# Pre-norm attention and an fp8 feed-forward on one core: softmax reciprocals by exp(-ln) on ACT, elementwise work of the rounds on DVE

## The chip, the core and the metric

The kernel runs on one core of a Trainium2 chip. A core has a matrix engine (TensorE, in the profile PE, with weight loads as PEld), a vector engine (VectorE, DVE), an engine for activation functions (ScalarE, ACT), a general one (GpSimd, POOL) and one that here only starts transfers (SyncE, SP). Each works through its own queue of instructions in order; semaphores tie the queues together. SBUF is the memory on the chip, PSUM the banks that TensorE writes. The metric is the device time of one execution in microseconds. The kernel before took 1808.78 us as the median of three runs (1807.12 to 1813.49).

## What is computed

```python
x = x + attention(layernorm(x))       # x: 2 x 2048 x 512, float32
x = x + ffn(layernorm(x))

# attention: 16 heads of 32, 2 groups of keys and values
q = rope(xn @ wq + bq) * 32 ** -0.5
k = rope(xn @ wk + bk); v = xn @ wv + bv
attn = softmax(q @ k.T * 32 ** -0.5)   # over 2048 keys
out = (attn @ v) @ wo + bo

# ffn: xn and the weight are each scaled to a maximum of 448 and rounded to e4m3
out = bf16((x_fp8 @ w_fp8.T) * (x_scale * w_scale))
```

The softmax is computed as a product of unnormalized probabilities with v, times the reciprocal of their sum.

## The kernel before

The 4096 tokens are 8 blocks of 512. Each block has 4 quads (4 heads each), and each quad two halves of 256 queries: 64 *units*. A unit goes through the 2048 keys of its batch in 16 chunks of 128, four chunks to a *round*, so there are 4 rounds in a unit and 256 in all.

In a round, `probabilities` (L969, L978, L987) does each chunk: TensorE writes the scores of 4 heads of a chunk into one of two PSUM tiles T (parity E or O), on top of the negated maxima of the queries for the first two chunks (the tile mT times `sel`, L969; later chunks add differences of keys to what stands in the tile), and ACT takes exp to SBUF as p. DVE adds p in pairs (`add_pair`, L961), an accumulating DMA issued from POOL's queue adds pair to pair (L991), and DVE joins what results (L994). TensorE multiplies p with the values one round later (`columns`, L924) and the joined sums with a tile of ones (`sum_up`, L942), which gives the sum of probabilities in the same layout as the values' product. Both lie in one tile `avs`, two buffers of it.

For the next unit, `first_scores` (L509, L517) and `gather_maxima` (L490, L529, L533) give the maxima of a first set of keys; the transposed maxima are copied by ACT to mT in the last round of a unit, between the second and the third chunk.

`finish_heads` (L890) ends a unit while the next one runs: ACT copies the sums out of PSUM (L895), DVE takes their largest bit pattern into `seen` (L897) and their reciprocal in two pieces (L903), POOL multiplies (L904) into `attn_of`. `seen` is compared with a bound at the very end (L1157); above it a slower general path would compute everything once more.

Beside the units run *jobs*, generators that yield ON_PE, ON_DVE, OTHER or LATER: the projection of keys and values of a later block (`project_kv`, `stack_keys`), of queries (`project_q`, `turn`, `rope`), the output product (`finish_block`), and the second norm. `fill` (called four times a round) takes the next piece of a job whose kind fits; LATER puts the rest off to the next round. The place of an instruction in each engine's queue is fixed by this order when the program is written out. `attending` is true in the rounds and false in the front part, which prepares the first keys and queries, and in the tail, which does the feed-forward.

In the rounds, these elementwise steps are on POOL: the two of `rope` (L325, L326), the difference `lo` in `halves` (L237), the difference of keys (L410), the copy of the old keys (L377), and var and mean of a norm (L196, L197). The normalizing of a block (`normalize`) is two activations on ACT in the rounds (L250, L253) and one DVE operation outside of them (L257).

Of the kernel before, what the change touches and what calls it, by code (L numbers as in the profile page):

```python
# [8 lines left out]
F32 = mybir.dt.float32  # L9
F32R = mybir.dt.float32r  # L10
BF16 = mybir.dt.bfloat16
U32 = mybir.dt.uint32
AF = mybir.ActivationFunctionType
ALU = mybir.AluOpType
AX = mybir.AxisListType

P = 128
# [3 lines left out]
TB = 512  # L21
NT = TB // P
EPS = 1e-5
# [4 lines left out]
def preln_attn_fp8_ffn_kernel(  # L28
# [37 lines left out]
    nc = tc.nc  # L66
# [9 lines left out]
    HB = 256  # L76
# [5 lines left out]
    ON_PE, ON_DVE, OTHER = "PE", "DVE", "other"  # L82
    LATER = "later"
# [101 lines left out]
    def layernorm_stats(src, mean, rstd, name, tiles=range(NT)):  # L185

        stats = small.tile([P, NT, 6], F32, tag="stats", name=f"stats_{name}")
        mv = small.tile([P, NT, 2], F32, tag="mv", name=f"mv_{name}")
        for i in tiles:
            yield ON_DVE  # L190
            nc.vector.bn_stats(stats[:, i, :], src[:, i, :])
            nc.vector.bn_aggr(mv[:, i, :], stats[:, i, :])
        at = slice(tiles[0], tiles[-1] + 1)
        var = small.tile([P, NT], F32, tag="var", name=f"var_{name}")
        engine = nc.gpsimd if attending[0] else nc.vector
        engine.tensor_scalar(var[:, at], mv[:, at, 1], EPS, None, ALU.add)  # L196
        engine.tensor_copy(mean[:, at], mv[:, at, 0])  # L197
        nc.gpsimd.tensor_tensor(rstd[:, at], var[:, at], neg_half[:, at], ALU.pow)
        if attending[0]:
            yield LATER  # L200
            yield OTHER
            yield LATER
# [15 lines left out]
    def round_e4m3(dst, v, magic):  # L218
# [10 lines left out]
        nc.vector.tensor_tensor(v, v, magic, ALU.add)  # L229
        nc.vector.tensor_tensor(dst, v, magic, ALU.subtract)  # L230

    def halves(src, rows, name):

        hi = t2(f"hi_{name}", F32R)
        lo = t2(f"lo_{name}", F32R)
        nc.scalar.copy(hi[:rows], src)
        nc.gpsimd.tensor_tensor(lo[:rows], src, hi[:rows].bitcast(F32), ALU.subtract)  # L237
        return hi, lo


# [3 lines left out]
    def normalized(n, xt, xnT, name):  # L244


        def normalize(i):
            if attending[0]:
                xn = t2(f"xn_{name}_{i}")
                nc.scalar.activation(  # L250
                    xn, xt[:, i, :], AF.Identity, bias=neg_mean[:, i : i + 1]
                )
                nc.scalar.activation(xn, xn, AF.Copy, scale=rstd1[:, n, i : i + 1])  # L253
                return xn
            else:
                xn = ppool.tile([P, 2, TB], F32, tag="p", name=f"xn_{name}_{i}")[:, 0, :]
            nc.vector.tensor_scalar(  # L257
                xn,
                xt[:, i, :],
                mean1[:, n, i : i + 1],  # L260
                rstd1[:, n, i : i + 1],
                ALU.subtract,
                ALU.mult,
            )
            return xn

        if attending[0]:
            neg_mean = small.tile([P, NT], F32, tag="neg_mean", name=f"neg_mean_{name}")
            nc.scalar.mul(neg_mean, mean1[:, n, :], -1.0)
        for i in range(0, NT, 2):  # L270
            xn = {}
            for h in (i, i + 1):
                yield OTHER if attending[0] else ON_DVE
                xn[h] = normalize(h)
            for h in (i, i + 1):
                yield ON_PE
                tp = bank(f"tp_{name}_{h}")
                for c in range(DC):
                    nc.tensor.transpose(
                        tp[:, c * P : (c + 1) * P], xn[h][:, c * P : (c + 1) * P], ident  # L280
                    )
                nc.scalar.copy(
                    xnT[:, :, h * P : (h + 1) * P], tp.rearrange("p (c t) -> p c t", c=DC)
                )
                give_back()
# [36 lines left out]

    def rope(dst, q, u, rows, csb):

        nc.gpsimd.tensor_tensor(q[:rows], q[:rows], csb[:rows, 0, :], ALU.mult)  # L325
        nc.gpsimd.tensor_tensor(dst, u[:rows], q[:rows], ALU.add)  # L326

# [34 lines left out]
    def project_kv(n, xt, xnT, csb):  # L364
        b, blk = divmod(n, NB)
        yield from layernorm_stats(xt, mean1[:, n, :], rstd1[:, n, :], f"1_{n}")
        yield from normalized(n, xt, xnT, f"kv_{n}")
        if n > 0:
            nc.sync.dma_start(xnT_far[n], xnT)
        if b not in vX:  # L370
            vX[b] = wide.tile([P, NTS, GROUPS, HD], F32, tag="vX", name=f"vX_{b}", bufs=2)
        pk = bank(f"pk_{n}")
        yield from product(pk, lambda c: wkv_sb[:, c, :], lambda c: xnT[:, c, :])
        if blk == 0:
            nc.gpsimd.memset(kx[:, :BACK], 0.0)
        else:
            nc.gpsimd.tensor_copy(kx[:, :BACK], kx[:, TB:])  # L377
        kv = t2(f"kv_{n}")
        nc.scalar.activation(kv, pk, AF.Identity, bias=bkv_sb)
        give_back()  # L380
        if attending[0]:
            u = swapped(kv, KD, f"k_{n}")
        else:
            u = yield from rotated(kv, csb, f"k_{n}")
        yield ON_PE
        tv = bank(f"tv_{n}")
        for i in range(NT):
            nc.tensor.transpose(tv[:, i * P : (i + 1) * P], kv[:, i * P : (i + 1) * P], ident)
        nc.scalar.copy(
            vX[b][:, blk * NT : (blk + 1) * NT, :, :].rearrange("p i g d -> p i (g d)"),  # L390
            tv.rearrange("p (i k) -> p i k", i=NT)[:, :, KD:],
        )
        give_back()
        if attending[0]:
            beside.insert(0, Job(stack_keys(n, kv, u, csb), due=step[0] + 2))
        else:
            yield from stack_keys(n, kv, u, csb)

    def stack_keys(n, kv, u, csb):
        b, blk = divmod(n, NB)  # L400
        if attending[0]:
            yield ON_DVE
            rotate(u, csb, KD)
        rope(kx[:, BACK:], kv, u, KD, csb)
        if attending[0]:
            table_users[0] -= 1
        cols = slice(blk * TB, (blk + 1) * TB)
        yield OTHER
        src = t2(f"dk_{n}")[:KD]
        nc.gpsimd.tensor_tensor(src, kx[:, BACK:], kx[:, :TB], ALU.subtract)  # L410
        if attending[0]:
            yield LATER
            yield OTHER
        far = halves_far["dkS", b]
        for h, part in enumerate(halves(src, KD, f"dkS_{n}")):
            nc.sync.dma_start(far[:, h, cols], part[:KD].bitcast(F32))
        if b == 0:
            far = far.rearrange("(g d) h t -> d h g t", g=GROUPS)
            stack(
                lambda rows: stacked["dkS"][rows, :, cols],  # L420
                [far[:, h, :, cols] for h in (0, 0, 1, 1)],
            )
        keys_done.add(n)
# [422 lines left out]
    def ask(u):  # L846
# [39 lines left out]
        if n == NBLK - 1 and quad == 3 and half == 0:  # L886

            fetch_y(4, wide, "qst", bufs=2)
            fetch_y_over_keys(5, "dkS", 0)

    def finish_heads(u, both, sums):

        k, half = units[u]
        n, quad = quads[k]
        nc.scalar.copy(both[:, 1, :], sums)  # L895
        yield ON_DVE
        nc.vector.tensor_reduce(  # L897
            seen[:, u : u + 1], both[:, 1, :].bitcast(U32), AX.X, ALU.max
        )
        for c in range(HB // P):  # L900
            yield ON_DVE
            piece = both[:, 1, c * P : (c + 1) * P]
            nc.vector.reciprocal(piece, piece)  # L903
        nc.gpsimd.tensor_tensor(  # L904
            attn_of[n][:, quad, half * HB : (half + 1) * HB], both[:, 0, :], both[:, 1, :], ALU.mult
        )
        if n == NBLK - 1:
            if quad == QUADS - 2 and half == HALVES - 1:
                queue.append(Job(finish_most(n, x_res[n], attn_of[n])))
            elif quad == QUADS - 1:  # L910
                queue.append(Job(finish_rest(n, x_res[n], attn_of[n], half)))
        elif quad == QUADS - 1 and half == HALVES - 1:
            job = Job(finish_block(n, attn_of.pop(n)))
            if n not in biased:
                job.due = NEVER
                without_x[n] = job
            queue.append(job)
# [90 lines left out]
        columns(u, chunks, probs, unit.avs[:, 0, :])  # L1008

    def keep_values(unit):  # L1010
        unit.both = w2.tile([P, 2, HB], F32, tag="both", name=f"both_{unit.u}", bufs=2)
        nc.scalar.copy(unit.both[:, 0, :], unit.avs[:, 0, :])  # L1012

    with tc.manual_schedule():
# [139 lines left out]
            ready = ahead  # L1154

    top = small.tile([P, 1], F32, tag="top", name="top")
    nc.vector.tensor_reduce(top, seen, AX.X, ALU.max)  # L1157
    across = bank("across_seen")
    nc.tensor.transpose(across[:1, :P], top, ident)
    flag = small.tile([1, 1], mybir.dt.int32, tag="flag", name="flag")  # L1160
# [264 lines left out]
```

## Time and profile before

| what | value |
|---|---|
| median of the runs | 1808.78 us |
| profiled execution, its own time | 1806.86 us |
| its span | 1805.0 us |
| granted clock of TensorE, mean | 0.966 |
| rounds | from about 92 to 1693 us |
| front part | about 92 us |
| tail | about 110 us |

Times in the profile are those of one execution on the chip. A line of a group of instructions gives the line of the source, the engine, the operation, what it writes and reads with the shapes, the count, the busy time with the mean of one in ns, and then the idle time of the engine just before them with what ended it. A line of the timeline gives the start, the length, the engine, and in brackets the idle time before it; instructions that follow one another are merged, so a length can hold several. A line of a stretch gives the stretch, its length, the busy time of PE, PEld, DVE, ACT and POOL with counts, the granted clock as a share of full speed, the DMA engines' share and GB/s. Matmuls overlap and their ends are modelled.

### The profile page before, as it was taken

The page shows a single profiled execution, that of the slowest core. Times are in us where ns is not written, and L with a number is a line of the kernel's source. Part 1 is how long each engine was busy: PE and PEld are TensorE (multiplying, and loading weights), DVE is VectorE, ACT ScalarE, POOL GpSimd, SP SyncE. Part 2 cuts the span into 40 slices and gives each one's busy share as a digit, 9 for nine tenths or more (in the row PEclk, how much of TensorE's full clock was granted, in tenths as well). Part 3 has the DMA queues.
Part 4 walks back from the last instruction along what each step waited for, and adds up shares of the span by engine and source line. Part 5 has one row for each costly group of instructions (what it writes and reads, how often), then busy time and mean ns, then how long its engine had stood idle before and what let it go on. Part 6 is the DMA issues. An engine that isn't in the chain of part 4 may idle for free.

```text
span 1805.0 us, 33804 instructions
## 1 busy us (share of the span) xinstructions
PE 1598.6 (89%) x13483; PEld 916.2 (51%) x13483; DVE 1315.7 (73%) x1526; ACT 1208.3 (67%) x1473; POOL 545.2 (30%) x552
## 2 busy tenths in 40 slices
PE   5588999899998999898999998999899988899664
PEld 3254555555555555555555554555555545555322
DVE  4547787767876787767768777787878787577697
ACT  2167677876767776776766777767777667566365
POOL 2333333244322532243314222332324223122100
PEclk9699999999999999999999999999999999999878
DMA  5676676767577866767588567766677558776222
GB/s 187 175 165 134 155 151 152 179 147 158 119 189 168 171 131 150 196 157 160 121 206 167 123 141 175 161 145 128 135 186 155 120 132 182 146 183 140 64 82 107
DMA packets 105431, 272.65 MB, mean 151 GB/s; under 512 B 15536, under 2 KB 16176, under 8 KB 102576
## 3 DMA queue, kind: packets, MB, share of 16 engines
q0 software_dynamic: 40944, 142.10, 42.1%
q1 hardware_dynamic: 61904, 126.92, 23.3%
q8 instruction: 108, 1.77, 0.4%
q10 hardware_dynamic: 2416, 1.38, 0.2%
q14 instruction: 59, 0.48, 0.1%
HBM read 87.36 MB, written 40.89 MB: 71 GB/s over the span
## 4 chain that ended last, share of the span: by engine, by line
PE 50%; DVE 14%; DMA 12%; issue 10%; ACT 7%; POOL 4%; SPq 2%; ACTq 0%; DVEq 0%; POOLq 0%
PE T L978 17%; PE avs L924 16%; DMA pa<-pa 9%; ACT p L987 6%; PE po L291 5%; DVE pa L961 4%; PE pq L291 3%; PE avs L942 2%; PE T L969 2%; DVE pa L994 2%; SPq L304 2%; DMA sw_q<-q 2%; PE pk L291 2%; PE s L509 1%; DVE v L229 1%
## 5 line engine op out<-in xcount | busy, mean ns | idle before, releaser
L987 ACT ACTIVATE p<-T 128x1024 f32<-128x1024 f32 x1024 | 991.9, 1023 | 218.1 <-PE T L978 214.3
L961 DVE TENSOR_TENSOR pa<-p,p 128x1024 f32<-128x1024 f32 x511 | 687.6, 1348 | 383.0 <-ACT p L987 273.2
L978 PE MATMUL T<-qst,dkS 128*128 128x512 f32 x2048 | 688.2, 446 | 44.8 <-ACT p L987 44.4
L991 POOL DMA_DIRECT2D pa<-pa x255 | 221.0, 867 | 971.8 <-DVE pa L961 671.6
L924 PE MATMUL avs<-p,vX 128*32 128x256 f32 x8192 | 497.3, 383 | 0.0
L978 PEld LDWEIGHTS T<-qst,dkS 128*128 128x128 f32 x2048 | 343.7, 191 | 285.2 <-ACT p L987 157.6
L924 PEld LDWEIGHTS avs<-p,vX 128*32 128x32 f32 x8192 | 240.4, 110 | 228.0 <-issue 96.5
L994 DVE TENSOR_TENSOR pa<-pa,pa 128x1024 f32<-128x1024 f32 x125 | 169.8, 1358 | 0.0
L291 PE MATMUL po<-wo_sb,attn 128*128 128x512 f32 x256 | 126.1, 604 | 0.0
L903 DVE RECIPROCAL both<-both 128x128 f32<-128x128 f32 x128 | 121.4, 949 | 5.6 <-DVE seen L897 0.5
L969 PE MATMUL T<-mT,sel 128*128 128x256 f32 x512 | 102.7, 324 | 11.2 <-ACT p L987 10.7
L291 PE MATMUL pq<-xnT_q,wq_sb 128*128 128x512 f32 x224 | 112.1, 607 | 0.0
L942 PE MATMUL avs<-pa,ones 128*32 128x256 f32 x1048 | 81.5, 385 | 28.7 <-DVE pa L994 27.7
L969 PEld LDWEIGHTS T<-mT,sel 128*128 128x128 f32 x512 | 78.0, 193 | 46.0 <-issue 20.6
L509 PEld LDWEIGHTS s<-dkS,qst 128*128 128x128 f32 x512 | 79.0, 196 | 22.2 <-DVE mx L517 10.9
L517 DVE TENSOR_REDUCE mx<-s 128x4 f32<-128x512 f32 x128 | 87.4, 683 | 2.8 <-PE s L509 2.8
L1012 ACT COPY both<-avs 128x256 f32<-128x256 f32 x64 | 23.9, 373 | 90.8 <-PE avs L942 88.1
L509 PE MATMUL s<-dkS,qst 128*128 128x128 f32 x512 | 74.4, 269 | 9.4 <-DVE mx L517 9.4
L904 POOL TENSOR_TENSOR attn<-both 128x256 f32<-128x256 f32 x64 | 78.9, 1232 | 9.7 <-DVE both L903 9.7
L895 ACT COPY both<-avs 128x256 f32<-128x256 f32 x64 | 23.9, 373 | 84.8 <-PE avs L942 84.8
L326 POOL TENSOR_TENSOR q<-sw_q,q 128x512 f32<-128x512 f32 x30 | 54.7, 1825 | 38.3 <-DVE sw_q L309 37.9
L533 ACT CAST mT<-mtp 128x256 fp32r<-128x256 f32 x64 | 23.8, 372 | 56.5 <-PE mtp L529 56.5
(124 smaller groups left out, 1075.5 us busy)
## 6 DMA issues: line engine op xcount, KB each, us to landing
pa<-pa POOLq DMA_DIRECT2D x255, 512.0 KB, 5.0
qst<-q_far SPq DMA_DIRECT2D x128, 256.0 KB, 4.9
q_far<-hi_q SPq DMA_DIRECT2D x32, 256.0 KB, 2.8
q_far<-lo_q SPq DMA_DIRECT2D x32, 256.0 KB, 3.4
x_res<-in_L_attn_x_dram SPq DMA_DIRECT2D x16, 512.0 KB, 7.2
x_res<-in_L_attn_bo_dram POOLq DMA_DIRECT2D x8, 1024.0 KB, 12.7
out_dram<-v SPq DMA_DIRECT2D x16, 512.0 KB, 2.8
sw_q<-q SPq DMA_DIRECT2D x240, 32.0 KB, 3.6
```

The costliest lines, as they stand in the source:

```text
L291: nc.tensor.matmul(dst, lhs(c), rhs(c), start=(c == 0), stop=(c == chunks - 1))
L509: nc.tensor.matmul(s[:, j, :], qst[k][:, j, at : at + P], stacked["dkS"][:, group(k), :FIRST], start=True, stop=True, skip_group_check=True,)
L517: nc.vector.tensor_reduce(mx[:, i, :], s, AX.X, ALU.max)
L903: nc.vector.reciprocal(piece, piece)
L924: nc.tensor.matmul(av[j * HD : (j + 1) * HD, :], vX[batch(k)][:, kc, group(k), :], p[:, j, :], start=(kc == 0), stop=(kc == NTS - 1), tile ...
L942: nc.tensor.matmul(dst[j * HD : (j + 1) * HD, :], ones, part[:, j, :], start=start and i == 0, stop=stop and i == len(parts) - 1, tile_pos ...
L961: nc.vector.tensor_tensor(pa, a, b, ALU.add)
L969: nc.tensor.matmul(T[:, j, :], sel[:, j, :], maxima[u], start=(j % 2 == 0), stop=True, skip_group_check=True,)
L978: nc.tensor.matmul(T[:, j : j + 2, :], stacked["dkS"][:, group(k), kc * P : (kc + 1) * P], qst[k][:, j : j + 2, half * HB : (half + 1) * H ...
L987: nc.scalar.activation(p, T, AF.Exp, scale=SCALE)
L991: nc.gpsimd.dma_start(out=to, in_=of, accum_op=ALU.add)
L994: nc.vector.tensor_tensor(to, to, of, ALU.add)
```

## The change

Three things change.

- `finish_heads` no longer uses DVE's reciprocal. ACT copies the sums and accumulates them along the row into `seen` in the same instruction. A round later ACT takes Ln of the sums s and Exp of its negative, which is a guess g of 1/s. Another round later DVE does a Newton step, (s g - 2) g, which is the negated refined reciprocal, and multiplies with the values and with -1. The tile `both` has three parts in place of two.
- The guard at the end takes the bit pattern of those row sums.
- In the rounds, what POOL did elementwise (the two rope operations, `lo`, the difference and the copy of keys, var and mean) is on DVE, and so is the normalizing, which ACT did in two activations. POOL keeps the power -1/2 of the variance, small operations of the second norm, and its DMA issues. The pieces concerned ask for a DVE slot (ON_DVE).

```diff
-        engine = nc.gpsimd if attending[0] else nc.vector
-        engine.tensor_scalar(var[:, at], mv[:, at, 1], EPS, None, ALU.add)
-        engine.tensor_copy(mean[:, at], mv[:, at, 0])
+        nc.vector.tensor_scalar(var[:, at], mv[:, at, 1], EPS, None, ALU.add)
+        nc.vector.tensor_copy(mean[:, at], mv[:, at, 0])
...
+    def elementwise():
+
+        return nc.vector if attending[0] else nc.gpsimd
+
     def halves(src, rows, name):
...
-        nc.gpsimd.tensor_tensor(lo[:rows], src, hi[:rows].bitcast(F32), ALU.subtract)
+        elementwise().tensor_tensor(lo[:rows], src, hi[:rows].bitcast(F32), ALU.subtract)
...
                 xn = t2(f"xn_{name}_{i}")
-                nc.scalar.activation(
-                    xn, xt[:, i, :], AF.Identity, bias=neg_mean[:, i : i + 1]
-                )
-                nc.scalar.activation(xn, xn, AF.Copy, scale=rstd1[:, n, i : i + 1])
-                return xn
...
-                yield OTHER if attending[0] else ON_DVE
+                yield ON_DVE
...
-        nc.gpsimd.tensor_tensor(q[:rows], q[:rows], csb[:rows, 0, :], ALU.mult)
-        nc.gpsimd.tensor_tensor(dst, u[:rows], q[:rows], ALU.add)
+        elementwise().tensor_tensor(q[:rows], q[:rows], csb[:rows, 0, :], ALU.mult)
+        elementwise().tensor_tensor(dst, u[:rows], q[:rows], ALU.add)
...
-            nc.gpsimd.tensor_copy(kx[:, :BACK], kx[:, TB:])
+            elementwise().tensor_copy(kx[:, :BACK], kx[:, TB:])
...
-        nc.gpsimd.tensor_tensor(src, kx[:, BACK:], kx[:, :TB], ALU.subtract)
+        elementwise().tensor_tensor(src, kx[:, BACK:], kx[:, :TB], ALU.subtract)
...
-        nc.scalar.copy(both[:, 1, :], sums)
+        av, total, guess = (both[:, i, :] for i in range(3))
+        nc.scalar.activation(total, sums, AF.Copy, accum_out=seen[:, u : u + 1])
+        yield LATER
         yield ON_DVE
-        nc.vector.tensor_reduce(
-            seen[:, u : u + 1], both[:, 1, :].bitcast(U32), AX.X, ALU.max
-        )
-        for c in range(HB // P):
-            yield ON_DVE
-            piece = both[:, 1, c * P : (c + 1) * P]
-            nc.vector.reciprocal(piece, piece)
-        nc.gpsimd.tensor_tensor(
-            attn_of[n][:, quad, half * HB : (half + 1) * HB], both[:, 0, :], both[:, 1, :], ALU.mult
+        nc.scalar.activation(guess, total, AF.Ln)
+        nc.scalar.activation(guess, guess, AF.Exp, scale=-1.0)
+        yield LATER
+        yield ON_DVE
+        nc.vector.tensor_tensor(total, total, guess, ALU.mult)
+        nc.vector.scalar_tensor_tensor(total, total, 2.0, guess, ALU.subtract, ALU.mult)
+        nc.vector.scalar_tensor_tensor(
+            attn_of[n][:, quad, half * HB : (half + 1) * HB], av, -1.0, total, ALU.mult, ALU.mult
         )
...
-        unit.both = w2.tile([P, 2, HB], F32, tag="both", name=f"both_{unit.u}", bufs=2)
+        unit.both = w2.tile([P, 3, HB], F32, tag="both", name=f"both_{unit.u}", bufs=2)
...
-    nc.vector.tensor_reduce(top, seen, AX.X, ALU.max)
+    nc.vector.tensor_reduce(top, seen.bitcast(U32), AX.X, ALU.max)
```

More of the change, by code (lines that the diff above doesn't have):

```diff
@@ L265, in normalize @@
             return xn
-        if attending[0]:
-            neg_mean = small.tile([P, NT], F32, tag="neg_mean", name=f"neg_mean_{name}")
-            nc.scalar.mul(neg_mean, mean1[:, n, :], -1.0)
         for i in range(0, NT, 2):
@@ L407, in stack_keys @@
         cols = slice(blk * TB, (blk + 1) * TB)
-        yield OTHER
+        yield ON_DVE
         src = t2(f"dk_{n}")[:KD]
-        nc.gpsimd.tensor_tensor(src, kx[:, BACK:], kx[:, :TB], ALU.subtract)
+        elementwise().tensor_tensor(src, kx[:, BACK:], kx[:, :TB], ALU.subtract)
         if attending[0]:
@@ L894, in finish_heads @@
         n, quad = quads[k]
-        nc.scalar.copy(both[:, 1, :], sums)
+        av, total, guess = (both[:, i, :] for i in range(3))
+        nc.scalar.activation(total, sums, AF.Copy, accum_out=seen[:, u : u + 1])
+        yield LATER
         yield ON_DVE
-        nc.vector.tensor_reduce(
-            seen[:, u : u + 1], both[:, 1, :].bitcast(U32), AX.X, ALU.max
-        )
-        for c in range(HB // P):
-            yield ON_DVE
-            piece = both[:, 1, c * P : (c + 1) * P]
-            nc.vector.reciprocal(piece, piece)
-        nc.gpsimd.tensor_tensor(
-            attn_of[n][:, quad, half * HB : (half + 1) * HB], both[:, 0, :], both[:, 1, :], ALU.mult
+        nc.scalar.activation(guess, total, AF.Ln)
+        nc.scalar.activation(guess, guess, AF.Exp, scale=-1.0)
+        yield LATER
+        yield ON_DVE
+        nc.vector.tensor_tensor(total, total, guess, ALU.mult)
+        nc.vector.scalar_tensor_tensor(total, total, 2.0, guess, ALU.subtract, ALU.mult)
+        nc.vector.scalar_tensor_tensor(
+            attn_of[n][:, quad, half * HB : (half + 1) * HB], av, -1.0, total, ALU.mult, ALU.mult
         )
```

## The prediction, made before the result was known

> **What bounds the kernel now.** I read the head of the page first, then the busy time of each engine by stretches of the span, then the waits, then the timeline of one unit's last round, and last the rows of the operations that the change touches.
>
> ```profile
> span 1805.0 us, 33804 instructions
> PE 1598.6 (89%) x13483; PEld 916.2 (51%) x13483; DVE 1315.7 (73%) x1526; ACT 1208.3 (67%) x1473; POOL 545.2 (30%) x552
> ```
>
> ```profile
> 80.00:300.00 220.00, 199.50 (x1671) 115.19 (x1671) 148.68 (x156) 152.41 (x188) 79.45 (x68) 0.97 0.63 138
> 700.00:900.00 200.00, 185.62 (x1591) 108.46 (x1590) 150.21 (x169) 141.69 (x172) 66.87 (x66) 0.98 0.71 161
> ```
>
> From 92 to 1693 us the 256 rounds run, and the second fence (columns: length, then busy PE, PEld, DVE, ACT, POOL, then granted clock) shows that TensorE is busy 93% of them, DVE 75%, ACT 71%, POOL 33%. TensorE is the bound; its idle time in all rounds adds up to 109 us. So an engine beside it matters only where it makes TensorE wait. That happens through the two score banks: a T of one parity can't be written before ACT's exponential of the last T of that parity has read it.
>
> ```profile
> L978 PE MATMUL T<-qst,dkS 128*128 128x512 f32 x2048 | 688.2, 446 | 44.8 <-ACT p L987 44.4
> L942 PE MATMUL avs<-pa,ones 128*32 128x256 f32 x1048 | 81.5, 385 | 28.7 <-DVE pa L994 27.7
> L529 PE MATMUL mtp<-ident,mrow 128*128 128x128 f32 x128 | 27.8, 299 | 5.7 <-DVE mrow L491 5.7
> L282 ACT ACT_TABLE_LOAD x1 | 1.3, 1283 | 9.9 <-DMA wkv_sb<-in_L_attn_wv_dram 9.9
> ```
>
> The idle time ahead of a group is the number behind its second bar. Before has one table load, 1283 ns long, at the start. Now the last round of a unit (here the one whose thirteenth exponential ends at 714.62), from the timeline:
>
> ```profile
> 712.68 1.94 ACT L987 ACTIVATE p<-T 128x1024 f32<-128x1024 f32 x2 [0.70 <-PE T L978]
> ...
> 715.02 1.17 PE L978 MATMUL T<-qst,dkS 128*128 128x512 f32 x4
> 715.30 0.37 ACT L533 CAST mT<-mtp 128x256 fp32r<-128x256 f32 x1 [0.69 <-PE mtp L529]
> 715.83 1.94 ACT L987 ACTIVATE p<-T 128x1024 f32<-128x1024 f32 x2 [0.15 <-PE T L978]
> 716.03 1.88 PE L291 MATMUL po<-wo_sb,attn 128*128 128x512 f32 x4
> 717.34 1.03 PE L969 MATMUL T<-mT,sel 128*128 128x256 f32 x4
> ```
>
> ACT finishes p12 and p13 at 714.62, idles 0.69, copies mT, and does p14 and p15 from 715.83. TensorE needs p14's bank at 717.34 for the next unit, and p14 ended at 716.85: 0.49 us of slack, and it is tight already at 0.05. Of the 63 such places in the trace, 43 have 0.49, 16 have 0.05, 4 more than 1.
>
> **The change, part by part.**
>
> *Ln and Exp on ACT.* The compiled list of the changed kernel has 128 table loads more than before: in each of the 64 units a load, Ln, a load, Exp (L896 and L897 of the changed file), and for nearly all they stand between p13 and the copy of mT, that is, in the stretch just shown. Exp of the probabilities needs no third load. Ln and Exp on 128x256 I take at 0.40 us each: a copy of 128x256 took 373 ns (L1012) and 128x1024 exponentials 1023 ns. Two loads at 1283 ns and two activations make 3.37 us. What queues behind them on ACT: mT, p14, p15, so the next unit's T. In the shown unit p14 would start 3.37 + 0.37 (mT) + 0.16 = 3.90 us after p13's end in place of 1.21, 2.69 us late; less 0.44 us of slack TensorE stops 2.2 us. Where slack is 0.05, p14 began 1.67 us after p13 (T came later), so the delay is 2.2 us again. Worked through the first 60 units with each one's own two numbers the stop sums to **122 us**; in six units it is under 0.8 us, three of them (p13 ends at 335.9, 539.7, 739.8) because the normalizing activations already hold ACT there. With a load that cost nothing the same sum gives 0, with one load 50. Nothing absorbs it later: TensorE is the bound and its order is fixed. What the trace can't show is the hand-over around a load inside a busy stretch. Lower bound nothing; upper bound the 0.29 us that ACT idles when it waits for TensorE (p at 701.13), at each of four hand-overs, 1.2 us a unit or 70 us. I take nothing, since back-to-back p's follow each other with no gap.
>
> The Trainium skill, "ScalarE: Activation LUTs", section What ACT_TABLE_LOAD costs, adds a drain of about 1380 ns to each load, 2.66 us a switch. By that the insertion is 6.1 us and the 60 units sum to 284, not 122. The same page, section Table sets: the hidden batching unit, says that ln then exp needs one load, because one set has both; by that the sum is 50 or less. The list of instructions has two per unit, and the only row has 1283 ns with nothing after it to show a drain, so neither is used.
>
> *The clock.* A stop of TensorE is followed in this trace by a lower clock. The trace has a trial of it at 338.8: ACT did two pairs of normalizing activations before p14, TensorE stood still 2.96 us, and the next stretches show it:
>
> ```profile
> 336.00:340.00 4.00, 2.34 (x22) 1.47 (x14) 3.18 (x3) 3.87 (x7) 1.13 (x2) 1.00 0.72 135
> 340.00:344.00 4.00, 2.71 (x14) 2.52 (x15) 1.23 (x1) 3.22 (x6) 0.88 (x1) 0.78 0.10 18
> 344.00:348.00 4.00, 4.00 (x45) 1.97 (x45) 0.32 (x1) 3.91 (x6) 1.27 (x1) 0.80 0.78 180
> ```
>
> The first T's of that unit took 3.35 us (341.70 to 345.05) against 2.45 (717.34 to 719.79), and the values' product 2.22 against 1.93: 1.2 us lost. The trace has 17 gaps over 1.5 us in the rounds and 10 stretches of half clock (3.4 us, two of 6.8), so about one gap in two. 57 new gaps x 0.5 x 1.2 = **34 us**; bounds 0 and 68.
>
> "TensorE: Matmul & The Clock Gate" in the Trainium skill, section Part 1: The HAM clock gate, lets the clock fall after an idle window of about 3.4 us. By that no stop of 2.2 us counts and these 34 us go; the 2.96 us gap above says otherwise.
>
> *Gone from DVE and POOL.* DVE loses 128 reciprocals (121.4 us) and 64 maxima (26.4). It gets 192 Newton and product operations of 128x256, at 0.43 us (by the line through 692 ns for 128x512 and 1225 for 128x1024, L229) 82 us; 60 rope operations on queries and 31 differences at 0.69, 63 us; 16 normalizations at 0.55, 9 us; keys some 12 us, var and mean 6. Net +24 us of 1316, on an engine with 25% idle. POOL loses L904 (78.9), L326, L325 and L237 on the rounds' queries and keys (some 160); its 255 accumulating DMA issues, which stand in the same queue, no longer stand behind these. SP's two q_far writes wait for DVE's lo in place of POOL's (0.7 against 1.5 us). DVE's rope waits for the swap's landing as before (17.8 us in all), now with two more operations behind it.
>
> What gets earlier: in the last two rounds DVE has 2.3 us less to do (maximum and reciprocals; the Newton step comes a round later, behind the first pair's sum, where DVE idles 1.1 to 1.9 us), so mrow, and the join ahead of the sums' product. These are TensorE's waits L942 28.7, L529 5.7, L509 8.7, and some 9 at L279 for ACT's normalizing: 52 us. I take two thirds, **-35**; bounds 0 and -52. POOL beside DVE also stretches DVE's sums (L961 mean 1348 ns, 1225 for the same shape in the tail), up to 80 us of DVE time; it is no bound, so I take nothing.
>
> *The rest at nothing.* The copy now also accumulates: it sits in 84.8/63 = 1.3 us of ACT idle (L895), which would hold a second copy. The 32 activations of 0.72 us that ACT loses lie in the three units named above and in the rounds beside them. The `both` tile has two buffers; the Newton step ends a round after the next one is taken, in the other buffer. Last three units and the tail: two more stops of 2.2 and a final chain of 5.0 us (copy, two loads, two activations, three DVE operations) against 3.9 (copy, maximum, two reciprocals, POOL's product), **+5**.
>
> Sum: 122 + 34 - 35 + 5 = +126 on the profiled execution's 1806.86, 1933; the median of the runs is 1.9 higher, so **1935 us**.
>
> **Rivals.**
> 1. *A switch costs far more than its row.* Each load also empties ACT, and the insertion nears 5 us. For it: p14 and p15 stand right behind, so nothing hides. Against: the row ends at 1283. At 70 us of hand-overs and every gap lowering the clock: 122 + 70 + 68 + 5 - 35 = +230, 2039; with 5 us of insertion (57 us of sum per us) about 2070.
> 2. *Only one load is paid* or part of it overlaps p13: 50, a clock term of 15 (shorter stops), - 35 + 5 = +35, 1844. Against it: two loads in the list, in program order on ACT.
> 3. *Faster: the loads don't hold ACT.* They copy while p13 runs, and only Ln and Exp (0.8 us) stand in the gap where ACT idles 0.69 anyway. Place: ahead of mT. Then the stop is 0 and DVE's and POOL's relief is what is left: 0 - 35 - 5 = -40, 1769. It decides below about 1.8 us of insertion, where 57 us of sum per us above 1.2 equals 35. For it only that the waits named exist; against it, the row shows the load as busy time of ACT.
>
> **How the numbers follow.** Forecast 0.79, first rival 0.11, second 0.06, third 0.04. Low end: 122 + 0 - 52 = +70, 1877. High end: the first rival's sum, 2039. The range 1872 to 2045 leaves out the third, the second and what of the first lies above 2045, under 0.2. A change within 0.3% (5.4 us, about what a measurement of this kernel can tell from none) needs the insertion to fall just at 1.8 us: 0.01. Faster 0.04, slower 0.95.
>
> **What would show it.** 129 table loads of 1283 ns; right after p13's end load, Ln, load, Exp, then mT, p14 some 3.9 us after p13; TensorE's idle time ahead of L967 (the sel product) from 11 us to over 90; more half-clock stretches; ACT near 1400 us busy, DVE near 1340 or under, POOL near 290; L940's wait mostly gone. Wrong if: a gap of a microsecond stands behind each load; TensorE finds work in the stop; or the accumulated sum lifts the guard over its bound and the general path runs behind everything else (sums of 256 terms against a bound of about 1e18: I give it no chance worth a number).

## The result, and the profile after

The changed kernel takes 1918.28 us (median of 4 runs, 1917.72 to 1925.02) against 1807.95 us for the kernel before (now the median of four runs): 1.0601 of before, 95% interval 1.0572 to 1.0629. Its profiled execution took 1918.67 us, with a span of 1916.8 us against 1805.0.

The head of the page of the changed kernel:

```profile
span 1916.8 us, 33427 instructions
PE 1626.9 (85%) x13478; PEld 925.8 (48%) x13483; DVE 1247.5 (65%) x1674; ACT 1399.1 (73%) x1757; POOL 304.8 (16%) x356
```

TensorE has the same matmuls and is 28.3 us longer busy; ACT got 191 us more, DVE 68 less, POOL 240 less. TensorE's groups, with the idle time ahead of each behind the second bar, and the new groups on ACT:

```profile
L976 PE MATMUL T<-qst,dkS 128*128 128x512 f32 x2048 | 696.6, 453 | 38.2 <-ACT p L985 37.9
L967 PE MATMUL T<-mT,sel 128*128 128x256 f32 x512 | 102.7, 329 | 107.4 <-ACT p L985 106.9
L286 PE MATMUL pq<-xnT_q,wq_sb 128*128 128x512 f32 x224 | 116.5, 622 | 20.4 <-ACT q L431 20.4
L940 PE MATMUL avs<-pa,ones 128*32 128x256 f32 x1048 | 80.3, 381 | 1.8 <-DVE pa L992 1.8
...
L896 ACT ACT_TABLE_LOAD x64 | 82.1, 1283 | 1.1
L897 ACT ACT_TABLE_LOAD x64 | 82.1, 1283 | 1.1
```

Two of these groups in the kernel before:

```profile
L969 PE MATMUL T<-mT,sel 128*128 128x256 f32 x512 | 102.7, 324 | 11.2 <-ACT p L987 10.7 <-ACT vX L389 0.5
L291 PE MATMUL pq<-xnT_q,wq_sb 128*128 128x512 f32 x224 | 112.1, 607 | 0.0
```

The wait ahead of the sel product of the next unit (L967; the product of mT and `sel` that opens its scores) went from 11 to 107 us. The wait for the joined sums (L940) went from 28.7 to 1.8. A wait of 20.4 us stands ahead of the query projection that wasn't there before. All of TensorE's idle time in the rounds sums to 189 us, against 106 for before, counted over the same stretch (first exponential to last): +82, and with the 28 us of longer busy time that makes +110, nearly the whole difference of the spans (111.8).

The last round of a unit, from the timeline of the changed kernel (start, length, idle time before it in brackets); the exponential p13 ends at 629.38:

```profile
628.35 1.03 ACT L985 ACTIVATE p<-T 128x1024 f32<-128x1024 f32 x1
629.39 1.28 ACT L896 ACT_TABLE_LOAD   x1
629.74 1.17 PE L976 MATMUL T<-qst,dkS 128*128 128x512 f32 x4
630.68 0.42 ACT L896 ACTIVATE both<-both 128x256 f32<-128x256 f32 x1
631.12 1.28 ACT L897 ACT_TABLE_LOAD   x1
632.41 0.42 ACT L897 ACTIVATE both<-both 128x256 f32<-128x256 f32 x1
632.74 0.35 ACT L528 CAST mT<-mtp 128x256 fp32r<-128x256 f32 x1
632.99 1.94 ACT L985 ACTIVATE p<-T 128x1024 f32<-128x1024 f32 x2
634.07 1.02 PE L967 MATMUL T<-mT,sel 128*128 128x256 f32 x4 [2.72 <-ACT p L985]
```

TensorE has p14's scores ready by 630.9, and p14 can't start before 632.99, because the five instructions ahead of it on ACT take 3.6 us. The next unit's sel product needs p14's bank and waits 2.72 us. In all 61 places with the loads ahead of mT, p14 begins 3.61 or 3.62 us after p13's end. The clock in the stretches around it (granted clock is the column before the last two):

```profile
630.00:634.00 4.00, 1.35 (x8) 0.89 (x7) 1.83 (x3) 3.96 (x7) 0.00 (x0) 1.00 0.76 142
634.00:638.00 4.00, 3.93 (x20) 2.99 (x24) 1.83 (x2) 3.04 (x6) 0.86 (x1) 0.57 0.26 97
638.00:642.00 4.00, 3.75 (x49) 2.34 (x39) 2.41 (x4) 2.39 (x4) 0.00 (x0) 1.00 1.04 176
```

After the stop the clock is at half for 3.4 us. In the rounds such stretches sum to 109 us in the changed kernel and 41 in the one before.

### The profile page after: what moved, and what is told of

The parts are those of the page before. It is cut to its first block, busy times and chain, and to the rows that moved or that the text cites. A ratio compares the mean times of both kernels' runs of the same rounds, so it can differ in the third digit from the quotient of the medians.

```text
span 1916.8 us, 33427 instructions
## 1 busy us (share of the span) xinstructions
PE 1626.9 (85%) x13478; PEld 925.8 (48%) x13483; DVE 1247.5 (65%) x1674; ACT 1399.1 (73%) x1757; POOL 304.8 (16%) x356
## 5 line engine op out<-in xcount | busy, mean ns | idle before, releaser
L959 DVE TENSOR_TENSOR pa<-p,p 128x1024 f32<-128x1024 f32 x511 | 624.5, 1223 | 575.7 <-ACT p L985 505.9
L976 PE MATMUL T<-qst,dkS 128*128 128x512 f32 x2048 | 696.6, 453 | 38.2 <-ACT p L985 37.9
L922 PE MATMUL avs<-p,vX 128*32 128x256 f32 x8192 | 508.1, 390 | 0.0
L976 PEld LDWEIGHTS T<-qst,dkS 128*128 128x128 f32 x2048 | 350.4, 194 | 271.5 <-ACT p L985 141.2
L967 PE MATMUL T<-mT,sel 128*128 128x256 f32 x512 | 102.7, 329 | 107.4 <-ACT p L985 106.9
L967 PEld LDWEIGHTS T<-mT,sel 128*128 128x128 f32 x512 | 82.6, 215 | 158.2 <-ACT p L985 143.0
L992 DVE TENSOR_TENSOR pa<-pa,pa 128x1024 f32<-128x1024 f32 x125 | 152.1, 1217 | 0.0
L286 PE MATMUL pq<-xnT_q,wq_sb 128*128 128x512 f32 x224 | 116.5, 622 | 20.4 <-ACT q L431 20.4
L1010 ACT COPY both<-avs 128x256 f32<-128x256 f32 x64 | 23.9, 373 | 97.3 <-PE avs L940 97.3
L896 ACT ACT_TABLE_LOAD x64 | 82.1, 1283 | 1.1
L897 ACT ACT_TABLE_LOAD x64 | 82.1, 1283 | 1.1
L940 PE MATMUL avs<-pa,ones 128*32 128x256 f32 x1048 | 80.3, 381 | 1.8 <-DVE pa L992 1.8
L893 ACT ACTIVATE both<-avs 128x256 f32<-128x256 f32 x64 | 24.6, 385 | 65.8 <-PE avs L940 65.8
L286 PEld LDWEIGHTS pq<-xnT_q,wq_sb 128*128 128x128 f32 x224 | 39.7, 194 | 43.3 <-ACT q L431 27.0
L274 PE MATMUL tp_kv<-ident,xn_kv 128*128 128x128 f32 x128 | 23.0, 320 | 43.4 <-DVE xn_kv L255 28.6
```

Source lines behind the costliest of these rows:

```text
L286: nc.tensor.matmul(dst, lhs(c), rhs(c), start=(c == 0), stop=(c == chunks - 1))
L896: nc.scalar.activation(guess, total, AF.Ln)
L922: nc.tensor.matmul(av[j * HD : (j + 1) * HD, :], vX[batch(k)][:, kc, group(k), :], p[:, j, :], start=(kc == 0), stop=(kc == NTS - 1), tile ...
L940: nc.tensor.matmul(dst[j * HD : (j + 1) * HD, :], ones, part[:, j, :], start=start and i == 0, stop=stop and i == len(parts) - 1, tile_pos ...
L959: nc.vector.tensor_tensor(pa, a, b, ALU.add)
L967: nc.tensor.matmul(T[:, j, :], sel[:, j, :], maxima[u], start=(j % 2 == 0), stop=True, skip_group_check=True,)
```

## The experiments

The theory: the two table loads a unit, ahead of p14, make the loss; TensorE stops, and the clock falls after the stop. The rivals: the work moved to DVE and the longer finish cost it; or a switch of tables costs much more than its row; or the clock's part is an accident of the trace.

**One table set.** The Trainium skill, "ScalarE: Activation LUTs", section Table sets: the hidden batching unit, says that `natural_log_exp_and_others` holds both exp and ln. Loaded once ahead of everything, it serves every activation of the kernel, and no other load is placed:

```diff
+    nc.scalar.preload_act_table_set("natural_log_exp_and_others")
     x_kv = {0: load_x(0, "kv")}
```

> The changed kernel with one table set, that holds both Ln and Exp, loaded once at the start; the 128 loads inside the units are gone, everything else stays. If the loads ahead of p14 make the 110 us: the insertion falls to two activations of 0.42 us, TensorE's wait ahead of the sel product falls from 107 us to about 10, and what is left is the relief of DVE and POOL: 1765 to 1785 us, faster than before. If the work moved to DVE (or the longer finish on three engines) costs most of it: 1860 us or more, with the wait ahead of the sel product small and others in its place.

It took 1784.72 us, 0.9898 of before (0.9861 to 0.9934), the upper end of the first case. Its lines for TensorE's waits:

```profile
L968 PE MATMUL T<-mT,sel 128*128 128x256 f32 x512 | 98.4, 314 | 12.9 <-ACT p L986 12.5 <-ACT vX L385 0.5
L941 PE MATMUL avs<-pa,ones 128*32 128x256 f32 x1048 | 80.8, 382 | 14.3 <-DVE pa L993 11.1 <-DMA pa<-pa 3.0
L287 PE MATMUL pq<-xnT_q,wq_sb 128*128 128x512 f32 x224 | 112.7, 604 | 10.5 <-ACT q L432 10.5
```

So 128 instructions of 1283 ns, 164 us of ACT's time, are worth about 130 us of the kernel's (1918.28 less 1784.72 is 134; by the ratios to before 7.0% or 127), and without them the change is a gain of 1%. The wait for the sel product is back at 13 us. Of the 20.4 us ahead of the query projection 10.5 are there without any load in the units, so only the other half comes from the loads. Half-clock stretches in the rounds are 38 us.

**One load and three loads.** Two more doses: in the kernel with one set a needless load of that set ahead of Ln (first diff), and in the changed kernel a third load between Ln and Exp (second diff).

```diff
+        nc.scalar.preload_act_table_set("natural_log_exp_and_others")
         nc.scalar.activation(guess, total, AF.Ln)
```
```diff
         nc.scalar.activation(guess, total, AF.Ln)
+        nc.scalar.preload_act_table_set("natural_log")
```

> The same, with one needless load of that set in each unit, ahead of Ln: the dose between. If TensorE's stop is proportional to what is inserted beyond ACT's 0.7 us of idle time: about 50 us of stops and 15 of clock over the run without loads, near 1835 us. If a load costs little as such and a change of the table's content is what is dear: within 10 us of the run without loads.

> The changed kernel with a third load (of the set of Ln once more) between Ln and Exp in each unit. If the stop grows with the insertion: 60 units x 1.28 us = 77 us and some 15 us of clock more than the changed kernel, near 2010 us. If something else starts to bound beside the stop (or takes part of it): under 1970 us.

One load: 1814.92 us, 1.0066 of before (1.0039 to 1.0092), 20 us under what was expected. Three: 2047.39 us, 1.1334 (1.1292 to 1.1377), 37 us over. The sel product's group in each, one load first:

```profile
L969 PE MATMUL T<-mT,sel 128*128 128x256 f32 x512 | 92.4, 304 | 37.3 <-ACT p L987 34.1 <-ACT vX L385 0.5
```
```profile
L968 PE MATMUL T<-mT,sel 128*128 128x256 f32 x512 | 130.0, 396 | 175.9 <-ACT p L986 175.4 <-ACT vX L384 0.5
```

The spans and sums in this table are those of one profiled execution each. The row without loads and the row with one are the kernel with one set.

| loads a unit | span us | wait ahead of sel, us | TensorE busy, us | half clock in the rounds, us |
|---|---|---|---|---|
| 0 | 1780.9 | 13 | 1591.5 | 38 |
| 1 | 1812.9 | 37 | 1599.2 | 41 |
| 2 (the change) | 1916.8 | 107 | 1626.9 | 109 |
| 3 | 2050.5 | 176 | 1679.3 | 246 |

The first load costs 32 us, since ACT idles ahead of mT and TensorE has some slack; the second 104; the third 134. The wait grows by 70 and 69 us for the second and third, near 60 x 1.28 = 77. What grows beyond it is above all the busy time of the same matmuls, 28 and 52 us, along with half clock: half of the added half-clock time is 34 and 68 us. The third load is of the table that is already there. Its rows have the same 1283 ns, and it costs no less than the second, so it is the instruction, not the change of content. The loads of the run with three:

```profile
L896 ACT ACT_TABLE_LOAD x64 | 82.1, 1283 | 1.2
L897 ACT ACT_TABLE_LOAD x64 | 82.1, 1283 | 1.1
L898 ACT ACT_TABLE_LOAD x64 | 82.1, 1283 | 0.3
```

The traces also show which stops lower the clock. Its changes lie on a grid of 3.41 us. Take each grid interval of the rounds that ran at full clock, and the share of it that TensorE was busy. In the changed kernel all 25 intervals with a share up to 0.40 were followed by one at half clock, and none of the 437 over 0.50 was; with three loads it was all 51 and none of 406. Between the two shares it went either way. A stop of 1.4 us leaves an otherwise full interval 0.59 busy: none of the 28 such stops of the changed kernel was followed by half clock, but 21 of its 28 gaps over 2.5 us were. So the third load, which takes most of the short stops from 1.4 to 2.7 us, costs more clock than the second.

**A filler in the stop.** To keep the clock up, needless matmuls into the free half of the bank of the transposed maxima, ahead of the sel product; first four a unit (the diff), then one.

```diff
+    spare = [None]
...
+        spare[0] = tp
...
                 fill(ON_DVE, 2)
+                if last and u + 1 < len(units):
+                    for _ in range(4):
+                        nc.tensor.matmul(
+                            spare[0][:, HB:], ident, wq_sb[:, 0, :HB], start=True, stop=True,
+                            skip_group_check=True,
+                        )
```

> The changed kernel with four needless 128x256 matmuls on TensorE (into the unused half of the bank of the transposed maxima) ahead of the next unit's sel product: 1.1 us of work a unit, 71 us in all, in the stop; the results don't use them. If the half clock after a stop costs time (109 us at half clock in the rounds): fewer half-clock stretches and 15 to 30 us less than the changed kernel, about 1895 us, in spite of the added work. If the clock costs nothing: 1918 us or, where the added work doesn't fit in the stop, up to 1940.

It took 1960.64 us, 1.0858 (1.0821 to 1.0894), outside of both expectations. The filler's own group tells why:

```profile
L1077 PE MATMUL mtp<-wq_sb,ident 128*128 128x256 f32 x504 | 144.7, 437 | 56.8 <-ACT mT L529 56.8
```

The 252 matmuls became 504 instructions and 145 us, twice what I had put, and they wait for ACT's copy of mT, since they write to its tile. They begin when only 1 us of the stop is left. The second version has one matmul a unit, with the changed kernel beside it on the same chip:

> The changed kernel with one needless matmul a unit in place of four (0.57 us each, from the first try), ahead of the sel product, where TensorE waits for p14; the results don't use it. If half clock after a stop costs time: fewer such stretches and 10 to 20 us under the changed kernel beside it on this chip. If it costs nothing: the same as the changed kernel, or up to 10 us more for what doesn't fit.

> The changed kernel itself, as a measure for the others on the same chip: 1.060 of before.

1918.58 us (1.0604, 1.0568 to 1.0640) beside 1921.38 us for the changed kernel (1.0619, 1.0587 to 1.0651). Half clock went from 113 to 85 us in the rounds, but the times can't be told apart, which is the second case. The filler still starts behind mT and leaves a wait of 56 us ahead of itself, so it tests only the last microsecond of the stop. What the clock costs is therefore not shown by these times; it rests on the busy time of the same matmuls. Beside the table above, the fillers bear it out: the score matmuls (T<-qst,dkS) average 453 ns in the changed kernel with 109 us of half clock in the rounds, 449 with one filler and 85 us, and 445 with four and 68 us.

**The two halves of the change apart.** The move alone (finish_heads, its tile and the guard as before; everything else as changed), and the reciprocals alone (the kernel before with the new finish_heads):

```diff
-        nc.scalar.activation(total, sums, AF.Copy, accum_out=seen[:, u : u + 1])
...
+        nc.scalar.copy(both[:, 1, :], sums)
...
+            nc.vector.reciprocal(piece, piece)
```

> Only the move of elementwise work (and of the normalizing) to DVE: the reciprocals are again two DVE operations with POOL's product behind them, as before. If the loads are the whole loss, this stands within 20 us of before (1790 to 1815 us): DVE gets some 95 us more work beside 25% idle time, TensorE loses its waits for ACT's normalizing. If the move costs: 1840 us or more.

> Only the reciprocals by Ln, Exp and a Newton step, with the guard; the elementwise work of the rounds stays on POOL and the normalizing on ACT. If the loads are the loss: 1915 to 1950 us, with the wait ahead of the sel product at about 100 us. If the move is the loss: under 1860 us.

The move alone: 1786.43 us, 0.9876 (0.9843 to 0.9909), 4 us under the first case. The reciprocals alone: 1953.89 us, 1.0799 (1.0766 to 1.0831), 4 us over the first case, with 104 us of wait ahead of the sel product. The third piece is the reciprocals alone with one table set:

> The reciprocals alone as in the last one, with one table set that holds Ln and Exp loaded once at the start. Beside the changed kernel with one set it gives the worth of the move to DVE without any load: if the relief comes from DVE losing the reciprocals, both stand within 10 us of one another, 1765 to 1790 us; if it comes from POOL's emptied queue, this one is near before, 1800 us or more.

1815.85 us, 1.0056 (1.0036 to 1.0076), the second case: near before. Put together, as shares of before:

| reciprocal | elementwise on POOL | elementwise on DVE |
|---|---|---|
| DVE, as before | 1 | 0.9876 |
| ACT, one set, no loads in the units | 1.0056 | 0.9898 |
| ACT, two loads a unit | 1.0799 | 1.0601 |

Read down, the loads cost 7% in either column, and the reciprocal on ACT without any load is no gain: 0.6% slower with the work on POOL, not to be told apart with the work on DVE. With the work on POOL the waits for the joined sums and for mrow do fall by 11 us (28.7 to 20.8 and 5.7 to 2.2), but 10.5 us ahead of the query projection come with the new `finish_heads`; the move alone has none there. Read across, the move gains 1.2 to 2.0% in each row.

**What in the move gains.** With the move alone, once with the normalizing back on ACT, and once with POOL's product of values and reciprocal on DVE too:

```diff
+                nc.scalar.activation(
+                    xn, xt[:, i, :], AF.Identity, bias=neg_mean[:, i : i + 1]
+                )
+                nc.scalar.activation(xn, xn, AF.Copy, scale=rstd1[:, n, i : i + 1])
...
```
```diff
-        nc.gpsimd.tensor_tensor(
+        nc.vector.tensor_tensor(
             attn_of[n][:, quad, half * HB : (half + 1) * HB], both[:, 0, :], both[:, 1, :], ALU.mult
```

> The reciprocals as before (DVE, with POOL's product), POOL's elementwise work of the rounds on DVE, but the normalizing back on ACT in two activations. If the gain of the move is POOL's queue and its contention with DVE: 1785 to 1792 us, as with the normalizing on DVE. If it is ACT's normalizing that leaves: 1800 us or more.

> The move alone (reciprocals as before), and POOL's product of values and reciprocal on DVE too, so that POOL has no elementwise work of the units left. 64 operations of 1.23 us leave POOL and 0.42 us each come to DVE: 1780 to 1788 us, at most a few us better than with the product on POOL. If DVE's load is what binds there: 1795 us or more.

1788.23 us (0.9889, 0.9862 to 0.9915) and 1790.10 us (0.9894, 0.9844 to 0.9943): both as the move alone, the second between its two cases. So the gain is not ACT's normalizing, and the last 64 operations on POOL add nothing to it. What is left is the rope, `lo`, the difference and the copy of keys, var and mean leaving POOL, with the places in the queues that this gives their pieces. In the move alone, DVE has as much to do as before (1319.8 us), while the sums of pairs got shorter (before first, then the move alone):

```profile
L961 DVE TENSOR_TENSOR pa<-p,p 128x1024 f32<-128x1024 f32 x511 | 687.6, 1348 | 383.0 <-ACT p L987 273.2 <-DMA pa<-pa 105.2 <-ACT both L1012 1.1
L958 DVE TENSOR_TENSOR pa<-p,p 128x1024 f32<-128x1024 f32 x511 | 633.4, 1242 | 349.3 <-ACT p L984 252.2 <-DMA pa<-pa 88.7 <-ACT q L431 3.7
```

1242 ns each against 1348 before, 54 us over 511 sums, with POOL at 363 us of work in place of 545. The trace of before shows where the stretch lies: the 361 of these sums that overlap no elementwise instruction on POOL average 1221 ns, and the 122 that overlap one by more than 0.5 us average 1696. Of the 21 us between the spans, 12 are TensorE's idle time in the rounds and 9 its busy time. Whether the shorter sums, POOL's shorter queue to its DMA issues or the new places of the pieces make the gain was not separated. With POOL's product on DVE too the sums are down to 1221 ns, and the time stays where it was. The versions that beat both kernels are these: the move alone, in any of its three forms, and the change with one table set, all 1.0 to 1.2% faster than before.

## Why the prediction came out right

The forecast was 1935 us with 1872 to 2045; the time is 1918. By its steps:

- **The insertion on ACT and TensorE's stop (122 us).** Right in mechanism and place, near in size. p14 starts 3.62 us after p13's end, where the working had 3.90: the copy of mT and p14 each begin about 0.1 us before the instruction ahead of them ends, where I had added 0.16. TensorE's waits show 96 us more ahead of the sel product, and 20 us ahead of the query projection, which the working doesn't have. Those are eight waits for ACT's copy of a projected query. Four of them, 3.7 us each, have the copy behind the loads, p14 and p15; with one set they are 1.28 us. The other four, 1.35 us each, are the same with and without loads. So the loads make some 10 of the 20 us, and the insertion 106 us where the working had 122. The stops are less even than the working's 2.2 us: 28 of 1.4 us and 26 of 1.7 to 3.1 us ahead of the sel product.
- **No cost at the hand-over around a load.** Shown: 10 to 20 ns (631.12 + 1.28 = 632.40, and Exp begins at 632.41). The first rival falls with it. The Trainium skill's drain of about 1380 ns a load, in "ScalarE: Activation LUTs", section What ACT_TABLE_LOAD costs, is in no row here. The 284 us that it would have made of the 122 were not paid.
- **The clock (34 us).** Busy time of the same matmuls grew by 28 us and half clock by 68 us, half of which is 34. That the size came out so near is in part luck. The working had every second of 57 stops lower the clock, at 1.2 us each; measured are 20 more grid intervals at half clock, at 1.4 us each, and the 28 stops of 1.4 us lowered it not once. The Trainium skill's rule of an idle window of about 3.4 us ("TensorE: Matmul & The Clock Gate", section Part 1: The HAM clock gate) would have left this term out; the gap of 2.72 us shown above was enough, and of the 25 intervals counted above (busy up to 0.40, all followed by half clock), three were busy 0.02 or less and the others 0.15 to 0.39. Three loads show that the term doesn't grow in proportion: there it is 52 us more for 1.28 us more of stop, where I expected 15.
- **The relief (-35 us).** The size was fair, its account wrong. The waits for sums and mrow went as said (28.7 to 1.8 and 5.7 to 0.5 us), but the wait ahead of the transposes, which I had counted as 9 us gained, rose from 36 to 43 us for the whole span. And the step that put the relief down to DVE losing its reciprocals fails: with one set and the work on POOL, where DVE has lost them, the kernel is 0.6% slower than before. The relief comes with the move, which alone is worth 22 us. The step "it is no bound, so I take nothing", for POOL's presence beside DVE, has the wrong size for DVE: its sums, which I said POOL stretches by up to 80 us, took 777 us in the changed kernel (L959 and L992) against 857, so that DVE ended at 1247 us busy and not near 1340. That the shorter sums are what TensorE gains from is not shown.
- **The rest (+5 us).** From the last exponential to the end it is 2.8 us longer. The accumulated copy brought a second instruction that reads the accumulator, 64 times 194 ns, in ACT's idle time.
- **The rivals.** One paid load, put at 1844 us, measures 1815 when it is made so; no load, put at 1769, measures 1785. They are 29 and 16 us off in opposite directions. The third's sum takes 5 us off for the rest, where the forecast adds 5, and gives no reason; with one set the stretch behind the last exponential is 1.8 us longer than before. The first rival's second figure, about 2070, comes to 2062 by its own terms. I read the two differences as a first load that is hidden better than the working had it (24 us of added wait ahead of sel, where it had 50) and a relief that is smaller where TensorE doesn't stop. The wait for the joined sums is 14 us without loads and 2 with two, so part of what looks like relief in the changed kernel is hidden under its stop.

## What to carry to other kernels

Price an instruction on an engine that isn't the bound by what stands behind it in its queue: here 3.4 us put between two exponentials made TensorE wait 1.6 us more a unit on average, and the longer of these stops also lowered its clock, in a stretch where ACT had 0.7 us to spare, though ACT was idle for a quarter of the span. Before a second function goes on ACT, read the list of table loads, and name a set that serves all functions if there is one: 128 loads were some 130 us. And when a change has two halves, measure each: here one gains 1.2%, and the other, even for free, nothing.

## What the runs showed that I had not expected

- Stops cost more than their length, and the more so the longer they are: going from two to three loads added 69 us to the wait ahead of the sel product and 134 us to the span. Half clock in the rounds went from 109 to 246 us. It is the busy share of a 3.41 us interval that decided: up to 0.40 the next was at half clock, in all 76 cases of these two traces, and over 0.50 never, in 843.
- Elementwise work on POOL slowed DVE: the sums of pairs took 1348 ns with it and 1242 ns (the move alone) to 1223 ns (the change) with less of it; in one and the same trace they took 1221 ns beside no such work and 1696 ns beside it. Taking 180 us of work from POOL and giving DVE the same steps, some 90 us by the working, left DVE's busy time where it was, at 1316 and 1320 us.
- A needless f32 matmul of 128x256 costs two instructions and 0.57 us, and here it waited for the reader of the other half of its tile.
